# Attention output by token: four heads in every step, or sixteen heads once a sequence

## The chip, the cores and the metric

The kernel runs on one core of one Trainium2 chip. The metric is the device time in microseconds of one execution; the time of a kernel is the median of several runs. All numbers in the profile are of one further, profiled execution.

## What is computed

One decoder layer for 16 sequences of 256 tokens with 256 channels, in three mixers, each with a layernorm ahead and a residual sum behind it. The change touches the first:

```python
qkv = jnp.einsum('bsd,ndh->bnsh', x, W_qkv)          # 16 heads of 16 channels
q, k, v = jnp.split(qkv, 3, axis=-1)
attn = jnp.einsum('bnqh,bnkh->bnqk', q, k) * scale   # causal mask, softmax over k
out = jnp.einsum('bnqk,bnkh->bnqh', attn, v)
out = out.reshape(B, -1, S)
return jnp.einsum('bds,nhd->bsd', out, W_out)
```

The reshape reads the heads' outputs in another order than the sums that follow, so W_out enters as one factor per row of the reshaped tensor, and the output has to be re-ordered. The second mixer is a gated linear attention over a context (scores times a decay matrix, times values, a norm per head). The third is a mixture of eight experts of which each token takes two.

## The kernel before, in words

Engines: TensorE (PE) multiplies matrices, VectorE (DVE) and ScalarE (ACT) empty PSUM and do the elementwise work, GpSimd (POOL) does selections and indirect DMAs, SyncE (SP) issues most DMAs.

**Order of the work.** First attention alone, then attention with the second mixer of the first eight sequences woven in, then the rest of the second mixer with the experts, then experts only. For the attention and what is woven into it, a list scheduler chooses each engine's order from the program's order and its own estimates of durations; every engine then executes its list in order, and waits at semaphores. From the expert part on, PE, ACT and SP are in the order in which the program is written.

**Attention.** A step k stands for a quad, four of the sixteen heads of one sequence: b, quad = divmod(k, 4). `attend_next(k)` emits: `maxima(k)` (scores ps_s at L370 and L375, and on VectorE twice `less` L384 and `off` L388, then L389, L390 and the transpose L393, whose rows SP copies into the queries); one quarter of the next sequence's preparation (`turn1` with ps_t L191, twice `project` with ps_qk L321, or `project_v` with ps_v L341); `weights(k - 2)` (transposed scores ps_st L411 and L415, exponential on ScalarE L419, causal selection on GpSimd L353); and `values(k - 4)` (ps_av L430 and L435, copied by ScalarE into avt, L439). The steps of a sequence are called first to fourth here: the first has `turn1`, the second and third `project`, the fourth `project_v`.

**by_token.** After the fourth quad's values of a sequence, `by_token(b)` turns all four quads of avt, whose one buffer holds a whole sequence, from channels-by-token to token-by-channel: for each half of 128 tokens four PE transposes into a ps_t tile (ps_o, L448), a reciprocal of the softmax sums (L453, 16 numbers a token), a product with the weights' sums (L454), and a multiplication of 16 x 16 numbers a token into `av` (L455). `av` holds eight sequences and has one buffer.

**reorder.** Behind the eighth sequence, `gather` (L472, L475) and `spread` (L480, L487) transpose av twice and add it to x.

**PSUM.** Pool ps_t has two buffers and serves ps_t, ps_qk, ps_v, ps_av, ps_o and most tiles of the second mixer (its values ps_h among them). Pool ps_p has three buffers of two banks; a step's ps_s takes two, its ps_st two, each taken round in turn.

**The weave.** `for k in range(k0)` runs attention alone. From k0 to `last`, every attend_next(k) is followed by an even share of the steps of gather, spread and the second mixer; they are all given out two steps ahead of `last`.

Of the kernel before, what the change touches and what calls it, by code (L numbers as in the profile page):

```python
# [12 lines left out]
F32 = mybir.dt.float32  # L13
# [3 lines left out]
ALU = mybir.AluOpType  # L17
# [3 lines left out]
P = 128  # L21
B, S, D = 16, 256, 256
NA, HA = 16, 16
NQ = NA // 4
NX, HX = 8, 32
E, FF = 8, 1024
SC = S // P
DC = D // P
FC = FF // P
GB = 8  # L30
UB = 4
TB = 256
HP = 32
# [37 lines left out]
def decoder_layer(  # L71
# [15 lines left out]
    nc = tc.nc  # L87
# [22 lines left out]
    ident = const.tile([P, P], F32, name="ident")  # L110
# [85 lines left out]
    ps_t = ctx.enter_context(tc.tile_pool(name="ps_t", bufs=2, space=PSUM))  # L196
# [25 lines left out]
    att = attention.enter_context(tc.tile_pool(name="att", bufs=2, side="right"))  # L222
# [46 lines left out]
    wq = const.tile([P, SC, NA], F32, name="wq")  # L269
# [22 lines left out]
    seq, quads = {}, {}  # L292
# [3 lines left out]
    def start1(b):  # L296
        mv = lstm.tile([P, SC, 2], F32, tag="mv1", name="mv1")
        rstd = lstm.tile([P, SC], F32, tag="rstd1", name="rstd1")
        statistics(b, mv, rstd)
        xn = lstm.tile([P, SC, D], F32, tag="xn", name="xn", bufs=3)  # L300
        normalized(xn, b, mv, rstd, nc.gpsimd if b else nc.vector)
        seq[b] = {"xn": xn}

    def turn1(b):
        xn = seq[b]["xn"]
        ps = transposed(ps_t, lambda c, dc: xn[:, c, dc * P : (dc + 1) * P])
        xnt = att.tile([P, DC, S], F32, tag="xnt", name="xnt", bufs=1)
        nc.scalar.copy(xnt, ps)  # L308
        seq[b]["xnt"] = xnt

    def project(b, half):


        xnt = seq[b]["xnt"]
        if half == 0:
            seq[b]["qt"] = att.tile([P, NQ, S], F32, tag="qt", name="qt")
        ps = ps_t.tile([P, 2, S], F32, tag="t", name="ps_qk")
        for i in range(2):
            n = (2 * half + i) * 4
            for dc in range(DC):  # L320
                nc.tensor.matmul(  # L321
                    ps[:, i, :],
                    lhsT=wqk_sb[:, dc, n : n + 4].rearrange("p n j h -> p (n j h)"),
                    rhs=xnt[:, dc, :],
                    start=dc == 0,
                    stop=dc == DC - 1,
                )
        part = slice(2 * half, 2 * half + 2)
        nc.scalar.copy(seq[b]["qt"][:, part, :], ps)
        for h in range(4):  # L330
            nc.sync.dma_start(
                out=ks[b % 2][HP * h : HP * h + HA, part, :],
                in_=seq[b]["qt"][HP * h + HA : HP * h + HP, part, :],
            )

    def project_v(b):
        xnt = seq[b]["xnt"]
        ps = ps_t.tile([P, SC, D], F32, tag="t", name="ps_v")
        for c in range(SC):
            for dc in range(DC):  # L340
                nc.tensor.matmul(  # L341
                    ps[:, c, :], lhsT=xnt[:, dc, c * P : (c + 1) * P], rhs=wv_sb[:, dc, :],
                    start=dc == 0, stop=dc == DC - 1,
                )
        nc.scalar.copy(vs[b % 2][:, :, :, :HA], ps.rearrange("p c (n h) -> p c n h", n=NA))

    def rows(h):
        return slice(HP * h, HP * h + HP)
# [53 lines left out]
    def weights(k):  # L402


        b, quad = divmod(k, NQ)
        kt, qt = ks[b % 2], seq[b]["qt"]
        p = att.tile([P, 4, 3 * P], F32, tag="p", name="p", bufs=PB)
        quads[k]["p"] = p
        ps, parts_ = four("ps_st")
        for h in range(4):  # L410
            nc.tensor.matmul(  # L411
                ps[h][:, :S], lhsT=kt[rows(h), quad, :P], rhs=qt[rows(h), quad, :], start=True, stop=True
            )
        for h in range(4):
            nc.tensor.matmul(  # L415
                ps[h][:, S:], lhsT=kt[rows(h), quad, P:], rhs=qt[rows(h), quad, P:], start=True, stop=True
            )
        for part, x_ in parts_:
            nc.scalar.activation(p[:, part, :], x_, AF.Exp, scale=1.0 / math.sqrt(HA))  # L419
        diagonals(p)  # L420

    def values(k):

        b, quad = divmod(k, NQ)
        p, v = quads[k]["p"], vs[b % 2]
        if quad == 0:
            seq[b]["avt"] = att.tile([P, NQ, S], F32, tag="avt", name="avt", bufs=1)
        pa = ps_t.tile([P, S], F32, tag="t", name="ps_av")
        for h in range(4):
            nc.tensor.matmul(  # L430
                pa[rows(h), :], lhsT=v[:, 0, 4 * quad + h, :], rhs=p[:, h, :S], start=True, stop=False,
                tile_position=(0, HP * h), skip_group_check=True,
            )
        for h in range(4):
            nc.tensor.matmul(  # L435
                pa[rows(h), P:], lhsT=v[:, 1, 4 * quad + h, :], rhs=p[:, h, S:], start=False, stop=True,
                tile_position=(0, HP * h), skip_group_check=True,
            )
        nc.scalar.copy(seq[b]["avt"][:, quad, :], pa)  # L439
        del quads[k]  # L440

    def by_token(b):

        avt = seq[b]["avt"]
        for c in range(SC):
            ps = ps_t.tile([P, NA, HP], F32, tag="t", name="ps_o")
            for quad in range(NQ):
                nc.tensor.transpose(  # L448
                    ps[:, 4 * quad : 4 * quad + 4, :].rearrange("p n h -> p (n h)"),
                    avt[:, quad, c * P : (c + 1) * P], ident,  # L450
                )
            rs = att.tile([P, NA], F32, tag="rs", name="rs")
            nc.vector.reciprocal(rs, ps[:, :, HA])  # L453
            nc.vector.tensor_tensor(rs, rs, wq[:, c, :], ALU.mult)  # L454
            nc.vector.tensor_tensor(  # L455
                avs[b // GB][:, c, :, b % GB, :].rearrange("p h n -> p n h"),
                ps[:, :, :HA], rs[:, :, None].to_broadcast([P, NA, HA]), ALU.mult,
            )
        del seq[b]

    def reorder(g):

# [574 lines left out]
    avs = {}  # L1037

    def attend_next(k):


        b, quad = divmod(k, NQ)
        if k < B * NQ:
            maxima(k)
        if b + 1 < B:
            if quad == 0:
                turn1(b + 1)
            elif quad < NQ - 1:
                project(b + 1, quad - 1)
        if 0 <= k - 2 < B * NQ:  # L1050
            weights(k - 2)
        if 0 <= k - 4 < B * NQ:
            done, part = divmod(k - 4, NQ)
            if done % GB == 0 and part == 0:
                avs[done // GB] = big.tile([P, SC, HA, GB, NA], F32, tag="av", name="av")
            values(k - 4)
        if b + 1 < B and quad == NQ - 1:
            project_v(b + 1)
        if 0 <= k - 4 < B * NQ and part == NQ - 1:
            by_token(done)  # L1060
        if quad == NQ - 2 and b + 2 < B:
            start1(b + 2)

# [5 lines left out]
    project_v(0)  # L1069
    output_sums()  # L1070
    nc.vector.tensor_scalar(gain, gain, 1.0, None, ALU.add)
    k0 = GB * NQ + 4
    last = B * NQ + 4

    def take(steps):
        f = steps.pop(0)
# [8 lines left out]
    for k in range(k0):  # L1085
        attend_next(k)
# [18 lines left out]
    for k in range(k0, last):  # L1105
        attend_next(k)
        take_evenly(steps, k + 1 - k0, last - k0 - EARLY)
# [236 lines left out]
```

## Time and profile before

| what | us |
|---|---|
| median of 6 runs (1218.35 to 1230.18) | 1220.68 |
| the profiled execution | 1227.71 |
| its span, first to last instruction | 1225.90 |
| PE busy | 1085.1 (89%) |
| DVE busy | 604.6 (49%) |
| ACT busy | 455.3 (37%) |
| POOL busy | 395.3 (32%) |

| group (L, engine) | count | mean ns |
|---|---|---|
| ps_o L448, PE, 128x128 | 128 | 273 (median) |
| rs L453, DVE, 128x16 | 32 | 257 (median) |
| av L455, DVE, 128x256 | 32 | 599 (median) |
| less L384, DVE, 128x512 | 128 | 678 |
| mxs L389, DVE, 128x1024 to 128x8 | 64 | 1208 |
| avt L439, ACT, 128x256 | 64 | 380 (median) |

A page of the profile gives each engine's busy time, the span in 40 slices, and groups of instructions by line. A timeline lists instructions in order of time; an idle time in brackets says how long the engine waited before one and what ended the wait. Matmuls are pipelined, so the lengths of neighbours overlap, and the starts are what to compare.

### The profile page before, as it was taken

The page shows a single profiled execution, that of the slowest core. Times are in us where ns is not written, and L with a number is a line of the kernel's source. Part 1 is how long each engine was busy: PE and PEld are TensorE (multiplying, and loading weights), DVE is VectorE, ACT ScalarE, POOL GpSimd, SP SyncE. Part 2 cuts the span into 40 slices and gives each one's busy share as a digit, 9 for nine tenths or more (in the row PEclk, how much of TensorE's full clock was granted, in tenths as well). Part 3 has the DMA queues.
Part 4 walks back from the last instruction along what each step waited for, and adds up shares of the span by engine and source line. Part 5 has one row for each costly group of instructions (what it writes and reads, how often), then busy time and mean ns, then how long its engine had stood idle before and what let it go on. Part 6 is the DMA issues. An engine that isn't in the chain of part 4 may idle for free.

```text
span 1225.9 us, 23326 instructions
## 1 busy us (share of the span) xinstructions
PE 1085.1 (89%) x8718; PEld 849.7 (69%) x8718; DVE 604.6 (49%) x1654; ACT 455.3 (37%) x928; POOL 395.3 (32%) x447
## 2 busy tenths in 40 slices
PE   5999999888989898874897859999879999999997
PEld 4677777655656565544675647777758899999996
DVE  4878777666776557525557553573611111111110
ACT  2345444435656552341385423744312111111111
POOL 5233332243534334535131153212542222222222
PEclk9799999978999886868789888999969999999999
DMA  6200000003113100125384455634648887788741
GB/s 189 61 19 13 17 14 17 10 6 109 62 33 126 62 23 27 54 97 217 130 313 149 147 174 182 220 113 138 192 147 298 304 291 248 241 295 258 243 134 22
DMA packets 61233, 165.44 MB, mean 135 GB/s; under 512 B 11584, under 2 KB 42176, under 8 KB 46784
## 3 DMA queue, kind: packets, MB, share of 16 engines
q1 hardware_dynamic: 47328, 144.45, 33.7%
q0 software_dynamic: 13248, 18.69, 7.6%
q8 instruction: 71, 1.16, 0.4%
q10 hardware_dynamic: 544, 0.79, 0.2%
q14 instruction: 42, 0.34, 0.1%
HBM read 136.30 MB, written 23.14 MB: 130 GB/s over the span
## 4 chain that ended last, share of the span: by engine, by line
PE 39%; DMA 13%; issue 10%; DVE 7%; ACT 4%; POOL 4%; another core or an unknown queue 1%; SPq 1%; POOLq 0%; DVEq 0%; ACTq 0%
PE ps_d L1215 11%; DMA out_x<-y,to 10%; PE ps_u L1197 9%; PE ps_h L651 3%; DMA rows<-table 2%; PE ps_t L191 2%; PE ps_sc L628 2%; PE ps_qk L321 2%; PE ps_st L411 2%; PE ps_s L370 1%; PE ps_av L430 1%; POOL out_x L1220 1%; DMA mb<-mm 1%; PE ps_r L1175 1%
## 5 line engine op out<-in xcount | busy, mean ns | idle before, releaser
L1197 PE MATMUL ps_u<-xt,up 128*128 128x128 f32 (+1 forms) x1536 | 258.8, 325 | 11.3 <-issue 9.6
L1215 PE MATMUL ps_d<-down,h 128*128 128x256 f32 x1088 | 254.5, 391 | 0.0
L1197 PEld LDWEIGHTS ps_u<-xt,up 128*128 128x128 f32 x1536 | 228.5, 194 | 36.8 <-issue 17.5
L1220 POOL DMA_INDIRECT out_x<-y,to x68 | 105.3, 1548 | 393.0 <-DVE y L1219 330.1
L1215 PEld LDWEIGHTS ps_d<-down,h 128*128 128x128 f32 x1088 | 210.5, 197 | 30.7 <-issue 2.0
L353 POOL TENSOR_SCALAR_AFFINE_SELECT p<-p 128x512 f32<-128x512 f32 x128 | 78.3, 635 | 200.7 <-ACT p L419 161.9
L419 ACT ACTIVATE p<-ps_st 128x768 f32<-128x768 f32 x128 | 99.1, 810 | 95.2 <-PE ps_st L415 93.9
L1203 ACT ACTIVATE h<-ps_u 128x512 f32<-128x512 f32 x78 | 46.6, 597 | 233.1 <-PE ps_u L1197 199.2
L1219 DVE TENSOR_SCALAR y<-ps_d,wt 128x256 f32<-128x256 f32 x68 | 32.8, 483 | 157.5 <-PE ps_d L1215 136.8
L384 DVE TENSOR_TENSOR less<-mask_a,ps_s 128x512 f32<-128x512 f32 x128 | 86.8, 678 | 42.5 <-PE ps_s L375 40.0
L411 PE MATMUL ps_st<-qt,kt 32*128 32x256 f32 x512 | 81.6, 468 | 24.3 <-DVE off L388 21.9
L370 PE MATMUL ps_s<-kt,qt 16*128 16x256 f32 x512 | 79.9, 440 | 10.8 <-DVE d L637 8.7
L321 PE MATMUL ps_qk<-xnt,wqk_sb 128*128 128x256 f32 x256 | 72.9, 434 | 8.3 <-ACT xnt L308 3.3
L850 POOL DMA_INDIRECT table<-x,place x64 | 63.6, 994 | 47.6 <-DVE place L846 21.6
L389 DVE TENSOR_REDUCE mxs<-less 128x8 f32<-128x1024 f32 x64 | 77.3, 1208 | 0.0
L353 POOL TENSOR_SCALAR_AFFINE_SELECT d<-d 128x512 f32<-128x512 f32 x64 | 39.9, 656 | 114.2 <-ACT d L619 76.8
L637 DVE SCALAR_TENSOR_TENSOR d<-ps_sc,d 128x384 f32<-128x384 f32 (+1 forms) x96 | 60.4, 681 | 23.8 <-PE ps_sc L632 13.8
L411 PEld LDWEIGHTS ps_st<-qt,kt 32*128 32x128 f32 x512 | 36.9, 204 | 50.8 <-issue 37.7
L619 ACT ACTIVATE d<-mb,at 128x256 f32<-128x256 f32 x128 | 63.7, 498 | 15.2 <-DMA mb<-mm 15.1
L182 POOL TENSOR_SCALAR xn<-x,mv,rstd 128x256 f32<-128x256 f32 x46 | 55.7, 1222 | 42.0 <-PE ps_t L191 27.3
L1177 DVE COPY xt<-ps_r 128x256 f32<-128x256 f32 (+1 forms) x48 | 25.6, 532 | 87.9 <-PE ps_r L1175 85.8
L321 PEld LDWEIGHTS ps_qk<-xnt,wqk_sb 128*128 128x128 f32 x256 | 52.2, 214 | 20.6 <-issue 3.8
(236 smaller groups left out, 1610.9 us busy)
## 6 DMA issues: line engine op xcount, KB each, us to landing
up<-in_wup SPq DMA_DIRECT2D x48, 1024.0 KB
down<-in_wdown SPq DMA_DIRECT2D x48, 1024.0 KB
mb<-mm SPq DMA_DIRECT2D x16, 1024.0 KB
rows<-table SPq DMA_DIRECT2D x20, 265.0 KB
x<-in_x SPq DMA_DIRECT2D x16, 256.0 KB
kt<-qt SPq DMA_DIRECT2D x128, 32.0 KB
qt<-rowed SPq DMA_DIRECT2D x256, 1.0 KB
cin<-in_ctx SPq DMA_DIRECT2D x16, 256.0 KB
```

Source lines behind the costliest of these rows:

```text
L321: nc.tensor.matmul(ps[:, i, :], lhsT=wqk_sb[:, dc, n : n + 4].rearrange("p n j h -> p (n j h)"), rhs=xnt[:, dc, :], start=dc == 0, stop=dc ...
L353: i = nc.gpsimd.affine_select(out=block, in_=block, compare_op=ALU.is_ge, fill=0.0, base=0, pattern=[[0, 4], [1, P]], channel_multiplier=-1,)
L370: nc.tensor.matmul(ps[h // 2][:, h % 2, P : P + S], lhsT=qt[channels(h), quad, P:], rhs=kt[channels(h), quad, :], start=True, stop=True,)
L384: nc.vector.tensor_tensor(less[:, part], mask_a[:, None].to_broadcast([P, 2, SC, P]), p.rearrange("p h (c k) -> p h c k", c=SC)[:, :, :, : ...
L389: nc.vector.tensor_reduce(mx[:, :, :4].rearrange("p c h -> p h c"), less, AX.X, ALU.min)
L411: nc.tensor.matmul(ps[h][:, :S], lhsT=kt[rows(h), quad, :P], rhs=qt[rows(h), quad, :], start=True, stop=True)
L419: nc.scalar.activation(p[:, part, :], x_, AF.Exp, scale=1.0 / math.sqrt(HA))
L619: nc.scalar.activation(d[:, h, :S], mb[:, n, :], AF.Exp, bias=at[:, 0, j, n : n + 1], scale=-1.0)
L850: i = nc.gpsimd.indirect_dma_start(out=table, out_offset=bass.IndirectOffsetOnAxis(ap=place, axis=0), in_=row, in_offset=None, bounds_chec ...
L1197: nc.tensor.matmul(ps[:, j, :], lhsT=m["up"][:, dc, f * P : (f + 1) * P], rhs=m["xt"][:, dc, :t], start=dc == 0, stop=dc == DC - 1,)
L1215: nc.tensor.matmul(ps, lhsT=m["h"][:, f, c * P : (c + 1) * P], rhs=m["down"][:, f, :], start=f == 0, stop=f == FC - 1)
L1220: a = nc.gpsimd.indirect_dma_start(out=acc, out_offset=bass.IndirectOffsetOnAxis(ap=m["to"][:, c : c + 1], axis=0), in_=y, in_offset=None, ...
```

## The change

values(k) writes avt for its own quad alone, into one of two buffers. by_token(k) handles one quad: two transposes, one for each half of the tokens, into one ps_o tile; one reciprocal and one product for both halves (8 numbers a token); and two multiplications of 4 x 16 numbers a token, for each half one. It is emitted in every step, one step behind its values (k - 5), so k0 and `last` grow by one.

```diff
@@ values
-        if quad == 0:
-            seq[b]["avt"] = att.tile([P, NQ, S], F32, tag="avt", name="avt", bufs=1)
+        avt = att.tile([P, S], F32, tag="avt", name="avt", bufs=2)
...
-        nc.scalar.copy(seq[b]["avt"][:, quad, :], pa)
-        del quads[k]
-
-    def by_token(b):
-
-        avt = seq[b]["avt"]
+        nc.scalar.copy(avt, pa)
+        quads[k] = avt
+
+    def by_token(k):
+
+        b, quad = divmod(k, NQ)
+        avt = quads.pop(k)
+        ps = ps_t.tile([P, SC, 4, HP], F32, tag="t", name="ps_o")
         for c in range(SC):
-            ps = ps_t.tile([P, NA, HP], F32, tag="t", name="ps_o")
-            for quad in range(NQ):
-                nc.tensor.transpose(
-                    ps[:, 4 * quad : 4 * quad + 4, :].rearrange("p n h -> p (n h)"),
-                    avt[:, quad, c * P : (c + 1) * P], ident,
-                )
-            rs = att.tile([P, NA], F32, tag="rs", name="rs")
-            nc.vector.reciprocal(rs, ps[:, :, HA])
-            nc.vector.tensor_tensor(rs, rs, wq[:, c, :], ALU.mult)
+            nc.tensor.transpose(ps[:, c].rearrange("p n h -> p (n h)"), avt[:, c * P : (c + 1) * P], ident)
+        part = slice(4 * quad, 4 * quad + 4)
+        rs = att.tile([P, SC, 4], F32, tag="rs", name="rs")
+        nc.vector.reciprocal(rs, ps[:, :, :, HA])
+        nc.vector.tensor_tensor(rs, rs, wq[:, :, part], ALU.mult)
+        for c in range(SC):
             nc.vector.tensor_tensor(
-                avs[b // GB][:, c, :, b % GB, :].rearrange("p h n -> p n h"),
-                ps[:, :, :HA], rs[:, :, None].to_broadcast([P, NA, HA]), ALU.mult,
-            )
-        del seq[b]
+                avs[b // GB][:, c, :, b % GB, part].rearrange("p h n -> p n h"),
+                ps[:, c, :, :HA], rs[:, c, :, None].to_broadcast([P, 4, HA]), ALU.mult,
+            )
+        if quad == NQ - 1:
+            del seq[b]
@@ attend_next
-        if 0 <= k - 4 < B * NQ and part == NQ - 1:
-            by_token(done)
+        if 0 <= k - 5 < B * NQ:
+            by_token(k - 5)
@@ the weave
-    k0 = GB * NQ + 4
-    last = B * NQ + 4
+    k0 = GB * NQ + 5
+    last = B * NQ + 5
```

## The prediction

> **What bounds the kernel now.** I read the page's slices first, then the busy time by stretches, then the instructions of VectorE and of TensorE over one sequence of the early attention, last the waits of the later part.
>
> ```profile
> PE   5999999888989898874897859999879999999997
> DVE  4878777666776557525557553573611111111110
> PEclk9799999978999886868789888999969999999999
> ```
>
> A slice is 30.6 us. Three parts show: up to about 245 us TensorE is at 9 and VectorE at 7 to 8; up to about 545 us no engine is full and the granted clock falls to 6 to 8; after 900 us TensorE alone counts. The stretches put numbers on it (columns: us, then PE, PEld, DVE, ACT, POOL busy with their instruction counts, then the clock, the DMA share, GB/s):
>
> ```profile
> 100.00:150.00 50.00, 48.22 (x560) 35.21 (x558) 38.35 (x88) 24.04 (x44) 17.05 (x24) 1.00 0.08 18
> 300.00:350.00 50.00, 48.48 (x562) 33.26 (x560) 36.00 (x75) 33.37 (x85) 24.14 (x32) 0.92 0.19 63
> 500.00:550.00 50.00, 40.30 (x346) 24.92 (x346) 18.16 (x51) 19.25 (x45) 25.97 (x29) 0.73 0.22 71
> ```
>
> In the attention alone TensorE looks full (48.2 of 50 at clock 1.00), but a busy row hides waits between matmuls, so I took one sequence step by step. VectorE first (start, length, instruction, in brackets the idle time before it):
>
> ```profile
> 118.61 0.69 DVE L384 TENSOR_TENSOR less<-mask_a,ps_s 128x512 f32<-128x512 f32 x1 [0.94 <-PE ps_s L375]
> ...
> 123.22 0.69 DVE L384 TENSOR_TENSOR less<-mask_a,ps_s 128x512 f32<-128x512 f32 x1 [1.04 <-PE ps_s L375]
> ...
> 128.49 0.26 DVE L453 RECIPROCAL rs<-ps_o 128x16 f32<-128x16 f32 x1 [1.71 <-PE ps_o L448]
> 128.79 0.17 DVE L454 TENSOR_TENSOR rs<-rs,wq 128x16 f32<-128x16 f32 x1
> 129.00 0.60 DVE L455 TENSOR_TENSOR av<-ps_o,rs 128x256 f32<-128x256 f32 x1
> ...
> 130.65 0.67 DVE L384 TENSOR_TENSOR less<-mask_a,ps_s 128x512 f32<-128x512 f32 x1
> ```
>
> The last row has no idle time ahead of it: `less` of the next sequence stood behind by_token's six instructions. TensorE in the same stretch:
>
> ```profile
> 123.13 0.70 PE L411 MATMUL ps_st<-qt,kt 32*128 32x256 f32 x4
> 124.39 0.48 PE L411 MATMUL ps_st<-qt,kt 32*128 32x256 f32 x2 [0.56 <-DVE off L388]
> ...
> 127.86 0.60 PE L448 MATMUL ps_o<-ident,avt 128*128 128x128 f32 x4
> 128.39 0.69 PE L370 MATMUL ps_s<-kt,qt 16*128 16x256 f32 x2
> 129.01 0.66 PE L448 MATMUL ps_o<-ident,avt 128*128 128x128 f32 x4
> ...
> 131.04 1.24 PE L411 MATMUL ps_st<-qt,kt 32*128 32x256 f32 x6
> ```
>
> A step without stalls is the second of the sequence, 113.14 to 117.64: ps_s 0.92, ps_qk 1.93, ps_st 0.87, ps_av 0.78. By these lengths the fourth step and the first of the next sequence need 2 x (0.92 + 0.87 + 0.78) + ps_v 1.83 + ps_t 0.58 + ps_o 0.53 and 0.59 = 8.67 us; they take 122.25 to 133.44 = 11.19. The 2.5 us over are 1.24 in the fourth step's ps_st (2.11), 0.56 in ps_s, which the second four transposes cut in two, and 0.74 in the first step's ps_st (1.61). The ps_st waits because its second PSUM tile is the one that `less` and `off` must empty (three tiles for two matmul groups), and `less` is late. A sequence takes 20.30 us (reciprocals at 128.49 and 148.79).
>
> **The change, part by part.** The sum is made against the profiled execution: 1227.71 us, span 1225.90, 1.81 outside it. The median of the six times is 1220.68, 7.03 less; I carry the difference over.
>
> (a) Attention alone, seven periods (reciprocals 67.57 to 210.33). Transposes stay 128, in 64 pairs; I take 0.33 a pair (half of 0.66 for four), 1.32 a sequence for 1.12: +0.2. VectorE does 16 instructions a sequence for 6: four times reciprocal 0.25, multiply 0.17, and two multiplies of 128x64. Those 128x64 are not in the trace with this striding; 0.22 is the row for 128x64 from PSUM (logit<-ps_lt, 218 ns), and a quarter of 0.60 gives 0.15 as the floor. 4 x 0.86 = 3.44 for 2 x 1.03 = 2.06: +1.4 us a sequence. VectorE's idle time there is 0.94 + 1.04 + 1.71 = 3.7, so it still fits. What counts is where it stands. The built order shows reciprocal, multiply, two multiplies directly ahead of every step's `less`, and ps_o at the end of the step or behind the next step's first ps_s matmul. In the first step, by_token's 0.86 then runs beside ps_s's 0.92: `less` can start when ps_s ends. `off` ends 1.0 later (130.65 to 131.65); TensorE has ps_t 0.58 and half of ps_st, 0.4, to do, so some 0.2 of the 1.30 over remain: -1.1. In the second and third steps `less` comes up to 1.1 us late, and ps_qk (1.93) ahead of ps_st covers it with 0.3 to spare. In the fourth the 1.24 stays: its `less` waits for ps_s either way. Net 0.2 - 1.1 = -0.9; seven times, **-6.3**. Ends: -16 if the whole 2.5 went (2.3 x 7), +10 if a narrow multiply cost the 0.60 of the wide one: VectorE's 15.6 busy (38.35 in 50, of 20.3) less 2.1, plus 4 x 1.62, plus its 1.7 of waiting for ps_o is 21.7 us a sequence.
>
> [...] The rows: 128x16 takes 175 ns, 128x256 with the same line's striding 600, so much of a small instruction is fixed. [...] The rows give +22 (1.4 x 16) and, beside them, the idle time that takes it.
>
> (b) Mixing begins one step later (k0 37 for 36), and the attention ends one later: one full step more alone (5.1), one less shared, and the last share of mixing meets a step that has only ps_av and ps_o. A shared step takes 10.9 (four in 290.04 to 333.81), the light ones at the end about 6: 5.1 - 10.9 + 6 = 0.2. Ends: -3, and +5 if mixing's own chain sets the stage's end. I take **+1.5**, for the clock of 0.73 at the end says that chains, not work, set it there.
>
> (c) The one buffer of `av`. by_token of the ninth sequence's first quad now comes ahead of the gathers that read the eighth's: it writes into the buffer they must empty. In the built order its ps_o stands ahead of 30 of the 32 gather transposes, its multiplies behind them all. So one of the two ps_t tiles is held for about a step, and ps_qk, ps_av and the next ps_o take turns in the other, each waiting for ScalarE's copy (0.58, 0.38). Queued behind on VectorE: the next reciprocal, x<-ps_x, `less`. The gathers' 24 transposes took 3.2 us (215.27). **+1.5**, ends 0 and +4.
>
> (d) Shared part, 245 to 545 us. Eight sequences with +1.4 on VectorE are 11 us. The chain of waits gives VectorE 7% of the span, 86 us of 605 busy, one seventh: **+1.5**; ends 0 and +11. ps_t, with two buffers, serves everything here; 16 more tenancies are emptied by VectorE. TensorE waited for `ct`, emptied from the same buffers, 2.4 + 0.6 + 0.2 in seven copies, 0.46 each: at most +7, **+1** taken, since avt is a step old and ACT avt and ACT v (1.1 and 2.0 us of weight-load waits) fall away. The burst ahead of `less` is halved here too: at most 8 x 1.1, **-1.5** taken, for most of these steps wait for other things.
>
> (e) The end: after the last ps_av eight transposes and six VectorE instructions, 541.5 to 543.3, become four and at most eight short ones: **-1**, ends -1.7 and 0. No DMA is added or moved by itself; SP's rows of extras follow `mxs`, which comes up to 1.1 us later in two steps and is used two steps on, and POOL's selections follow ScalarE.
>
> Sum: -6.3 + 1.5 + 1.5 + 1.5 + 1 - 1.5 - 1 = -3.3. Profiled 1224.4, median **1217.4 us**. What follows 545 us waits for the attention's memory and keeps its length: I count the stage's end one for one.
>
> **Rivals.** *Both stages gain* (0.20): if the shared part's waits of ps_st for `off` (15.2 us in 11) go like those of the alone part, -6 more with (b) at 0.2: -10 to -14, 1208.7. For: VectorE idles 20.2 us in seven waits for ps_o there. Against: TensorE is at 48.5 of 50 in 300 to 350 with little to give. *The shared part loses* (0.28): an in-order VectorE reaches a reciprocal before its ps_o is done, twice as often, and the ps_t buffer behind it stops ps_h and ps_qk. Price: 11 + 7 less (a)'s 6.3 and about 3 of overlap, +9: 1229.7. It decides once a shared sequence grows by 0.8 us (6.3 / 8). For: waits of 4.2, 2.7, 2.0 and 7.3 us for ps_o stand in that part now. Against: a step's lag makes ps_o ready early. *It doesn't smooth* (0.10): in the alone part VectorE becomes the loop once a narrow multiply costs 0.4 (15.6 - 2.1 + 4 x 1.22 + 1.7 = 20.1): the period stays 20.3, and (b) to (e) remain: +3, 1223.7. Against: every 128x64 row is under 0.45. My forecast has 0.42, own range 1211 to 1224.
>
> **How the numbers follow.** About 0.5%, 6.1 us, is what a measurement can tell from no change. Faster: the first rival 0.20 and a quarter of the forecast's 0.42, 0.31. Slower: the second rival and a little of the third, 0.30. Between: 0.39. The range reaches from the first rival's far side (1206) over the second's price with two thirds of (b)'s bound, 1232.
>
> **What would show it.** Reciprocal to reciprocal of the same quad in the alone part: 19.4 us for 20.3 (right), 20.3 (third rival). ps_s uncut and ps_st of the first step near 1.1; the fourth step's ps_st still 2.1. 128x64 multiplies near 0.22. First cin transposes within 2 us of now (247.09): (a)'s gain goes into the later begin of (b). Last ps_o at about 539 us for 542.2. I am wrong if a 128x64 multiply costs 0.4 or more, or if the waits for ps_o in the shared part pass 35 us.

## The result and the profile after

The changed kernel takes 1230.67 us against 1222.89 for the kernel before: a ratio of 1.0072, 95% interval 1.0054 to 1.0090. That is slower, by 8 to 9 us (7.8 between the medians, 8.8 by the ratio), where a gain of 3 was forecast. The profiled execution took 1231.74 us, its span is 1230.0 (before: 1227.71 and 1225.9). These two spans lie only 4.1 us apart: the traces show where time moved, and the ratio of the timed executions says how much was lost.

The slices of the page after (30.7 us each):

```profile
PE   5999999998999898976688768999979999999997
DVE  5778888766766756526447553474612111111110
PEclk9799999977988985678799888999969999999999
```

VectorE's digits are nearly those of before. The clock's row has 5, 6, 7 where before has 6, 8, 6, from 460 to 550 us. The busy time by stretches, and then of the whole shared part up to the first of the experts' matmuls (columns: us, then PE, PEld, DVE, ACT, POOL busy with their instruction counts, clock, DMA share, GB/s):

```profile
100.00:150.00 50.00, 47.66 (x568) 33.99 (x566) 41.64 (x115) 24.16 (x44) 17.06 (x24) 1.00 0.08 18
300.00:350.00 50.00, 48.90 (x548) 33.60 (x544) 36.01 (x84) 32.10 (x79) 23.82 (x31) 0.88 0.21 66
500.00:550.00 50.00, 40.28 (x350) 22.61 (x342) 18.98 (x70) 16.30 (x37) 29.93 (x33) 0.67 0.22 76
245.00:560.30 315.30, 278.83 (x2543) 177.38 (x2540) 188.42 (x538) 145.13 (x357) 135.15 (x157) 0.79 0.18 59
```

The same last row of the kernel before, whose shared part ends at 551.9:

```profile
245.00:551.90 306.90, 263.50 (x2568) 175.15 (x2568) 184.41 (x462) 145.40 (x353) 131.22 (x154) 0.82 0.18 60
```

In the first row VectorE has 3.3 us more work in 50, as forecast (1.4 a period of 20.3). By the last row of each kernel the shared part is 8.4 us longer. TensorE's idle time there did not grow, it fell (306.9 - 263.5 = 43.4; 315.3 - 278.8 = 36.5). What grew is its busy time, by 15.3 us, for nearly the same matmuls (2543 records for 2568), and VectorE's by 4.0. The mean granted clock is lower, 0.79 for 0.82. A second execution of the changed kernel, on another chip (after_again below), has the longer part and the busier TensorE too, but not the lower clock:

```profile
245.00:558.80 313.80, 273.87 (x2578) 177.05 (x2577) 192.70 (x551) 146.45 (x359) 135.29 (x157) 0.82 0.18 59
```

**The alone part** gained nothing: 20.39 us a sequence (first matmul of ps_s 149.22 to 169.61) for 20.41 before (148.69 to 169.10). Its steps now take 4.14, 4.44, 5.89 and 5.92; before 5.05, 4.51, 4.66 and 6.19. VectorE over the first step of one sequence:

```profile
149.32 0.21 DVE L450 RECIPROCAL rs<-ps_o 128x8 f32<-128x8 f32 x1 [1.50 <-PE ps_o L447]
149.56 0.17 DVE L451 TENSOR_TENSOR rs<-rs,wq 128x8 f32<-128x8 f32 x1
149.76 0.40 DVE L453 TENSOR_TENSOR av<-ps_o,rs 128x64 f32<-128x64 f32 x2
150.18 0.69 DVE L384 TENSOR_TENSOR less<-mask_a,ps_s 128x512 f32<-128x512 f32 x1
```

The reciprocal starts where the forecast wanted it and `less` 0.86 later: this step gained 0.91. But the gain is not where the forecast had most of it. TensorE in the same step:

```profile
149.22 0.71 PE L370 MATMUL ps_s<-kt,qt 16*128 16x256 f32 x8
...
150.08 0.66 PE L191 MATMUL ps_t<-ident,xn 128*128 128x128 f32 x4
150.67 1.17 PE L411 MATMUL ps_st<-qt,kt 32*128 32x256 f32 x6
...
152.20 0.64 PE L429 MATMUL ps_av<-p,v 128*32 128x256 f32 x8
```

ps_s, no longer cut, and ps_o take 0.86 and 0.37 us for 2.06 together before; ps_st takes 1.53 for 1.62, where the forecast wanted 1.1. The third step lost the gain again. TensorE there, and under it the weight load of the same two transposes:

```profile
157.80 0.69 PE L370 MATMUL ps_s<-kt,qt 16*128 16x256 f32 x2
158.52 0.44 PE L447 MATMUL ps_o<-ident,avt 128*128 128x128 f32 x2
158.88 0.49 PE L370 MATMUL ps_s<-kt,qt 16*128 16x256 f32 x3
...
165.83 0.48 PE L411 MATMUL ps_st<-qt,kt 32*128 32x256 f32 x2 [0.78 <-DVE off L388]
```

```profile
158.51 0.20 PEld L447 LDWEIGHTS ps_o<-ident,avt 128*128 128x128 f32 x2 [0.42 <-ACT qt L329]
```

ps_o needs a ps_t tile that ScalarE's copy `qt` must free (157.88 to 158.46, behind an exponential), and stands in the middle of ps_s: ps_s to ps_qk takes 1.94 us there, for 0.92 uncut and 1.09 in the third step of the kernel before. A second ps_o falls into the same step (163.32 to 163.69). The two, 0.85 and 0.37, are the 1.23 us that this step is longer. The fourth step's ps_st still waits for `off`, as forecast.

**VectorE's waits in the shared part**, from the view of waits, for the changed kernel from 245 to 560 us:

```profile
DVE rs L450 <- PE ps_o L447: 47.5, 19, 6.4
DVE den L674 <- ACT den L673: 11.3, 7, 5.1
DVE r L557 <- ACT r L556: 10.7, 2, 6.4
DVE less L384 <- PE ps_s L375: 10.6, 8, 2.2
```

and for the kernel before, to 552 us:

```profile
DVE rs L453 <- PE ps_o L448: 20.2, 7, 7.3
DVE less L384 <- PE ps_s L375: 14.2, 11, 4.3
```

47.5 us in 19 waits for 20.2 in 7: the prediction's sign of its own failure (35 us) is passed. The last ps_o is at 550.3 us, not 539.

### The profile page after: what moved, and what is told of

The parts are those of the page before. It is cut to its first block, busy times and chain, and to the rows that moved or that the text cites. A ratio compares the mean times of both kernels' runs of the same rounds, so it can differ in the third digit from the quotient of the medians.

```text
span 1230.0 us, 23465 instructions
## 1 busy us (share of the span) xinstructions
PE 1098.3 (89%) x8718; PEld 847.4 (69%) x8718; DVE 619.4 (50%) x1814; ACT 455.6 (37%) x928; POOL 394.9 (32%) x447
## 4 chain that ended last, share of the span: by engine, by line
PE 53%; DMA 16%; issue 10%; DVE 10%; ACT 6%; POOL 3%; another core or an unknown queue 1%; SPq 1%; POOLq 0%; ACTq 0%; DVEq 0%
DMA out_x<-y,to 12%; PE ps_d L1214 9%; PE ps_u L1196 8%; PE ps_qk L321 5%; PE ps_st L411 4%; PE ps_s L370 4%; PE ps_h L650 4%; PE ps_v L341 3%; PE ps_av L429 3%; PE ps_t L191 2%; PE ps_sc L627 2%; PE ps_o L447 2%; DMA rows<-table 2%; PE ps_st L415 1%
## 5 line engine op out<-in xcount | busy, mean ns | idle before, releaser
L1214 PE MATMUL ps_d<-down,h 128*128 128x256 f32 x1088 | 251.7, 388 | 0.0
L384 DVE TENSOR_TENSOR less<-mask_a,ps_s 128x512 f32<-128x512 f32 x128 | 86.9, 679 | 20.2 <-PE ps_s L375 19.7
L370 PE MATMUL ps_s<-kt,qt 16*128 16x256 f32 x512 | 85.5, 464 | 6.5 <-DVE d L636 5.3
```

What stands on the lines that cost most here:

```text
L370: nc.tensor.matmul(ps[h // 2][:, h % 2, P : P + S], lhsT=qt[channels(h), quad, P:], rhs=kt[channels(h), quad, :], start=True, stop=True,)
L384: nc.vector.tensor_tensor(less[:, part], mask_a[:, None].to_broadcast([P, 2, SC, P]), p.rearrange("p h (c k) -> p h c k", c=SC)[:, :, :, : ...
L1214: nc.tensor.matmul(ps, lhsT=m["h"][:, f, c * P : (c + 1) * P], rhs=m["down"][:, f, :], start=f == 0, stop=f == FC - 1)
```

## Experiments

Each is compared with the kernel before on the same chip. They fell on four chips. On two the kernel before takes 1224 to 1227 us, on two 1179 to 1181: the profiled kernels need 630 to 635 us behind the attention on these two, for 670 to 675, whatever the attention did. So ratios are compared, and kernels on one chip above others. `EARLY` (2 in both kernels) is the number of steps ahead of `last` by which the shares are all given out.

### Shift, start and lag, one at a time

**shift_only**: the kernel before, mixing and end one step later.

```diff
-    k0 = GB * NQ + 4
-    last = B * NQ + 4
+    k0 = GB * NQ + 5
+    last = B * NQ + 5
```

> The kernel before, sixteen heads at once, with k0 and last one higher: the weave begins one attention step later and nothing else changes. Theory S (the weave's later begin): the woven mixer's own chain sets the end of the shared part, so a step alone (5.1 us) is added in full: ratio 1.004 to 1.007, first cin transposes 5 us later, periods of the attention alone unchanged at 20.4 us. Theory V (VectorE's ten more short instructions a sequence in the shared part): nothing of them is here, so 0.999 to 1.002. Theory P (twice as many ps_o tiles in the two-buffer pool): 0.999 to 1.002.

Measured 0.9938 [0.9909, 0.9966]: a gain where every theory had none or a loss. The forecast's (b), +1.5, has the wrong sign, and theory S (the later begin itself costs) falls.

**begin36**: the changed kernel with the mixing begun where it was before, in the same 30 shares.

```diff
-    k0 = GB * NQ + 5
+    k0 = GB * NQ + 4
-EARLY = 2
+EARLY = 3
```

> The changed kernel with the weave begun at step 36 again, as before the change, and its shares spread over the same 30 steps; by_token stays by four heads and one step behind. S: the loss goes, ratio 0.997 to 1.002, last ps_o at 541 to 545 us. V and P: the loss stays, 1.005 to 1.009.

Measured 1.0029 [0.9994, 1.0065]: between what S had (up to 1.002) and what V and P had (from 1.005). On this one chip the split is 0.9% behind shift_only; VectorE waits for ps_o 38.7 us in 19.

**split_nolag**: the changed kernel with by_token in its values' own step.

```diff
-        if 0 <= k - 5 < B * NQ:
-            by_token(k - 5)
+        if 0 <= k - 4 < B * NQ:
+            by_token(k - 4)
```

(k0 and `last` as in the kernel before.)

> By four heads, but directly behind the values of the same step; k0 and last as before. S: no shift, 0.998 to 1.003. V and P: all the short instructions and all 64 ps_o tiles are here, 1.005 to 1.009; if only the lag costs, about 1.000. In the attention alone ps_o must wait for ScalarE's avt copy (0.38 us) in each step, unless TensorE has ps_s to do meanwhile.

Measured 1.0339 [1.0287, 1.0391], the alone period 23.2 to 26.7 us, 55.1 us of waits for ps_o in 24. The split without the lag is far worse.

**lag_only**: sixteen heads at once as before, one step later.

```diff
-            seq[b]["avt"] = att.tile([P, NQ, S], F32, tag="avt", name="avt", bufs=1)
+        avt = att.tile([P, S], F32, tag="avt", name="avt", bufs=5)
+        seq[b].setdefault("avt", []).append(avt)
...
-        if 0 <= k - 4 < B * NQ and part == NQ - 1:
-            by_token(done)
+        if 0 <= k - 5 < B * NQ and k % NQ == 0:
+            by_token((k - 5) // NQ)
```

(k0 and `last` one later.)

> Sixteen heads at once as before, but emitted one step later (k0 37, last 69), with five one-quad avt tiles in place of the one of four quads. S: 1.004 to 1.007, as for the weave's later begin alone. V and P: 0.999 to 1.002, for the instructions are those of before.

Measured 0.9891 [0.9852, 0.9930]; no theory had a gain here either. The two parts of the change that are not the split are worth 0.6 to 1.1%, and the split takes more than that.

### Count, time and waits

**after_again**: the changed kernel, beside the next three.

> The changed kernel again, as the reference of the kernels run beside it, for the chip of the first experiments was faster than the first one in the expert part. If the change costs the same there: ratio 1.005 to 1.010 and some 25 us more than the lag alone. Theory S has fallen: the later begin alone gained. Left are V (the short instructions on VectorE), P (an in-order VectorE waits for more ps_o tiles, and ps_t tiles wait for it) and O (the order that the list scheduler arrives at).

Measured 1.0081 [1.0041, 1.0121].

**pairs**: eight heads every second step, with the lag.

```diff
-        ps = ps_t.tile([P, SC, 4, HP], F32, tag="t", name="ps_o")
+        ps = ps_t.tile([P, SC, 8, HP], F32, tag="t", name="ps_o")
...
-        if 0 <= k - 5 < B * NQ:
+        if 0 <= k - 5 < B * NQ and (k - 5) % 2:
```

> Eight heads every second step: half the dose of the change, 8 VectorE instructions a sequence for 6, two ps_o tiles a sequence as before the change, and the lag of one step and k0 37 as changed. V and P: at most a third of the split's cost is left, so near the lag alone, 0.989 to 0.996. O: no order by dose, anywhere from 0.985 to 1.01.

Measured 1.0009 [0.9981, 1.0037], with 18.7 us of waits for ps_o in 7. Half the split lies between the whole and none in time; V and P had 0.989 to 0.996 for it. In waits it is like the kernel before.

**dve_more**: lag_only, with a reciprocal and a multiplication of 8 and 16 columns of avt added in every step; their results are used by nothing.

```diff
+            nc.vector.reciprocal(w, seq[b_]["avt"][q_][:, :8])
+            nc.vector.tensor_tensor(y, seq[b_]["avt"][q_][:, :16], seq[b_]["avt"][q_][:, 64:80], ALU.mult)
```

> The lag alone (sixteen heads), with two short VectorE instructions added in each step that read the avt tile and that nothing uses (8 a sequence, about 1.5 us, as many as the split adds in time). V: the cost of the split comes back without its ps_o tiles: 1.000 to 1.010. P: hardly any, 0.988 to 0.995.

Measured 1.0073 [1.0043, 1.0103], 1.5 to 1.8% above the two measurements of lag_only (on other chips). VectorE in the alone part:

```profile
122.83 0.20 DVE L1063 RECIPROCAL w<-avt 128x8 f32<-128x8 f32 x1 [1.37 <-ACT avt L439]
122.95 0.36 DVE L1064 TENSOR_TENSOR w<-avt 128x16 f32<-128x16 f32 x1
123.23 0.68 DVE L384 TENSOR_TENSOR less<-mask_a,ps_s 128x512 f32<-128x512 f32 x1
```

and its waits from 245 us to the end of the stage:

```profile
DVE w L1063 <- ACT avt L439: 36.3, 19, 6.7
```

No PSUM tile and no matmul was added, so a cost of this size needs no ps_o tile. Instructions whose result nobody reads, and which wait for another engine at the head of VectorE's queue, cost about what the split costs. Not all in the same place: the alone period is 21.35 us here for 20.44 in lag_only, some 6 us in seven sequences, and there the split lost nothing.

**act_evict**: the changed kernel, with ps_o copied to SBUF by ScalarE and VectorE's part one step later.

```diff
+        tok = att.tile([P, SC, 4, HP], F32, tag="tok", name="tok", bufs=2)
+        nc.scalar.copy(tok, ps)
+        quads[k] = tok
+
+    def by_token2(k):
...
+        if 0 <= k - 6 < B * NQ:
+            by_token2(k - 6)
```

(`last` one later, `EARLY` 3.)

> The changed kernel, but ScalarE copies ps_o into SBUF and VectorE's part follows one step later: no VectorE instruction waits for a ps_o tile and none holds one, and all 16 VectorE instructions stay. 64 copies of 0.38 us are added on ScalarE; weave begin at 37 as changed. P: the split's cost goes, 0.985 to 0.998, and the alone period falls under 20 us unless ScalarE's copies come late. V: the cost stays, 1.005 or more.

Measured 1.0186 [1.0149, 1.0223]; the alone period is 24.0 to 24.1 us and VectorE waits 54.0 us in 22 for `tok` in the shared part. The wait was not removed, it changed its name, so this kernel cannot tell P from V.

### The time of the instructions, and the order

**lag_again**: lag_only once more, beside the next three.

> The lag alone (sixteen heads) again, beside the runs below and on their chip: 0.987 to 0.993 if the gain doesn't hang on the chip.

Measured 0.9922 [0.9878, 0.9966].

**dve_own**: lag_only, with two short multiplications in 59 of the steps that read only what VectorE itself wrote; their results are used by nothing.

```diff
+            nc.vector.tensor_tensor(w, mx[:, 0, :8], mx[:, 1, :8], ALU.mult)
+            nc.vector.tensor_tensor(y, mx[:, 0, :16], mx[:, 1, :16], ALU.mult)
```

> The lag alone with two short VectorE multiplications added in each of 59 steps that nothing uses, as before with the ones that read avt, but here they read what VectorE itself has just written in that step (the negated maxima), so they wait for no other engine. V (their time): the 1.8% between the lag alone and the run whose added instructions read avt comes back, 1.003 to 1.010. H (an instruction at the head of VectorE's queue that waits for another engine holds back less, d and all else behind it): at most 0.3% comes back, 0.988 to 0.994.

Measured 0.9982 [0.9944, 1.0020], 12.7 us of waits for ps_o in 5. That is between V (from 1.003) and H (to 0.994). Against lag_again it is 0.6%, some 6 us, with intervals that overlap, for 11.7 us more of VectorE's busy time (612.2 for 600.5); dve_more added 19.8 (621.5 for 601.7 in lag_only). So time alone seems to cost less than waiting, but it isn't shown to cost nothing: at this price the 14.8 us that the split adds to VectorE would be some 8.

**shift2**: the kernel before with k0 and `last` two later.

> The kernel before with the weave begun two steps later (k0 38, last 70). If a later begin helps by itself (less attention beside the mixing), the gain grows or holds, 0.988 to 0.994. O (the order that the list scheduler happens on): 0.985 to 1.01, no trend after 0.994 for one step.

Measured 1.0053 [1.0029, 1.0078]. One step later gains 0.6%, two lose 0.5%.

**early1**: the kernel before with its shares ended one step later.

```diff
-EARLY = 2
+EARLY = 1
```

> The kernel before with the mixing's steps spread over 31 attention steps in place of 30 (EARLY 1), which adds and removes no instruction: it shows how far a mere re-ordering moves the time. O: over 0.5% in either direction. If orders matter little: 0.997 to 1.003.

Measured 0.9854 [0.9808, 0.9899] (0.9911 when measured again, below), with no instruction added or removed. The order in which the scheduler happens to set the same work is worth -1.5 to +0.5%.

### The split in three weaves

All kernels of the split but split_nolag and begin36 begin the mixing one step later than the kernel before (k0 37 for 36). Of those with sixteen heads at once, shift_only and lag_only with all that was made from it do so too; early1 and early3 do not.

**after_early1**: the changed kernel with `EARLY` 1.

> The changed kernel with the mixing spread over 31 steps (EARLY 1), the re-ordering that moved the kernel before to 0.985. If the split costs something of its own beside the luck of the order: 0.990 to 1.000, behind the kernel before in the same weave by 0.5 to 1.5%. If the 0.7% was luck alone: 0.980 to 0.990.

Measured 1.0027 [0.9996, 1.0059], a little above what either theory had.

**after_early3**: the changed kernel with `EARLY` 3.

> The changed kernel with the mixing spread over 29 steps (EARLY 3). A cost of its own: above the kernel before in the same weave (run beside it) by 0.5 to 1.5%. Luck alone: on either side of it.

Measured 1.0056 [1.0031, 1.0081].

**early3**: the kernel before with `EARLY` 3.

> The kernel before with the mixing spread over 29 steps (EARLY 3): a further order of the same instructions. Luck of the order: anywhere from 0.985 to 1.010.

Measured 0.9984 [0.9952, 1.0016], 22.1 us of waits for ps_o in 7, where after_early3 on the same chip has 47.1 in 22.

**before_values**: the changed kernel with by_token emitted ahead of the step's `weights`.

```diff
+        if 0 <= k - 5 < B * NQ:
+            by_token(k - 5)
         if 0 <= k - 2 < B * NQ:
             weights(k - 2)
```

(and not at its old place)

> The changed kernel with by_token(k - 5) emitted ahead of weights(k - 2) in the step, so that ps_o stands between ps_qk (or ps_s) and ps_st and doesn't follow ps_av. If in the attention alone the gain of the first step was lost to ps_o's waits in the second (for the ps_t tile that ScalarE's copy of ps_qk must free) and to the cut ps_s: the period falls from 20.4 to 19.0 to 19.9 us. If VectorE's 16 instructions are the loop there: 20.2 or more. The time as a whole is open to the luck of the order, 0.99 to 1.01.

Measured 1.0301 [1.0244, 1.0358]; the alone period is 21.3 to 22.1 us, where 19.0 to 19.9 was hoped for. TensorE there:

```profile
126.84 0.64 PE L429 MATMUL ps_av<-p,v 128*32 128x256 f32 x8 [1.22 <-DVE av L453]
```

by_token's VectorE part now stands behind the maxima, so it holds a ps_t tile until 126.7, and ps_av waits for it. Its waits of VectorE for ps_o are only 15.3 us in 8, less than before the change: that sum alone does not rank the kernels.

**early1_again** and **lag_early1**: the kernel before, and lag_only, each with `EARLY` 1, on one chip.

> The kernel before with EARLY 1, again: the shares of the second mixer end one step later, so 31 of them for 30, and by_token as before. What is still open is whether its gain (0.9854, on the chip whose expert part is shorter) is a property of the weave or of that chip. Theory O (the order that the scheduler happens on): 0.980 to 0.991 on either chip, stage's end 10 to 20 us ahead of that of the kernel before, waits of VectorE for ps_o in the shared part again 14 to 22 us in 7 or 8. If it was that chip: 0.995 to 1.005. With the changed kernel at 1.0027 in the same weave on the other chip, O with a cost of the split (H, P) has the split at 1.2 to 2.2% here too; if the cost of the split was only luck, the two come within 0.5%.

> Sixteen heads once a sequence as before, one step later, with EARLY 1: the two edits that gained by themselves together (0.9891 and 0.9922; 0.9854). If a gain of each came from its own stall, they add: 0.974 to 0.982. If both are only other orders that the scheduler happens on (O), the sum means nothing: 0.985 to 1.000. H and P expect only that the waits for ps_o stay under 22 us, as in every kernel with sixteen heads at a time, and that it stays ahead of the changed kernel with EARLY 1 (1.0027) by 1% or more.

Measured 0.9911 [0.9881, 0.9940] and 0.9919 [0.9889, 0.9949]. The gains do not add, so they are not two separate stalls removed; orders that happen to suit, or one stall that both edits remove, are left. Both beat both kernels by about 1%, as does lag_only.

### TensorE's clock in all of them

The granted clock is the share of full speed that TensorE was given. Looked at in steps of 1 us, as thirteen of the twenty traces were, it is 1.00 or 0.50, and nothing between but where it changes. The changed kernel, one microsecond a row:

```profile
297.00:298.00 1.00, 0.10 (x2) 0.00 (x0) 0.00 (x0) 1.00 (x5) 0.90 (x2) 1.00 0.01 1
298.00:299.00 1.00, 0.00 (x0) 0.00 (x0) 0.64 (x1) 1.00 (x4) 1.00 (x2) 0.69 0.00 0
299.00:300.00 1.00, 0.54 (x2) 0.53 (x4) 1.00 (x2) 1.00 (x5) 1.00 (x2) 0.50 0.00 0
...
305.00:306.00 1.00, 1.00 (x20) 0.81 (x24) 0.00 (x0) 0.01 (x1) 0.00 (x0) 0.90 0.07 18
```

TensorE stands still for some 2 us, the clock halves within the second one (0.69 is the mean) and comes back 6.8 us later. From 245 us to the end of the shared part, every such stretch in the twenty traces lasts 3.4 us or a multiple (3.4, 6.8, 10.2, 13.6 ...); in the seven others that is read from rows of 5 us. In the changed kernel, from 100 us to 243 us the clock is 1.00 throughout. The longest stretch of the changed kernel:

```profile
466.00:502.00 36.00, 32.38 (x208) 20.19 (x200) 21.66 (x81) 7.07 (x17) 11.34 (x13) 0.50 0.06 20
```

The kernel before has 23.9 us there (from 465), lag_only 20.5.

Not every fall has such a gap ahead of it: at 335.92 the clock fell after 3.4 us (332.50 to 335.92) in which TensorE was busy for 3.31 by its records. That was four 128x128 transposes and, up to the first of ps_av in the last 0.1 us, matmuls of 16 and 32 rows. What makes the clock fall is not shown.

What a microsecond at half clock costs can be estimated from equal programs: over the timed runs of the kernel before on each of the four chips (22 to 29 runs), the span grows by 0.34 to 0.38 us for each us more of it (correlation 0.82 to 0.95). The estimate takes the clock for the cause of this scatter, which no run shows. Time at half clock is here 2 x (1 - mean granted clock) x span. With 0.36 for the price, means over the timed runs, against the kernel before on the same chip:

| kernel | span, us | at half clock, us | x 0.36 | rest |
|---|---|---|---|---|
| after_again | +9.7 | +31 | +11.3 | -1.5 |
| shift_only | -6.9 | -1 | -0.4 | -6.4 |
| lag_only | -13.6 | -11 | -4.0 | -9.6 |
| begin36 | +3.4 | +14 | +5.1 | -1.8 |
| after_early3 | +7.4 | +30 | +10.8 | -3.4 |
| early3 | -2.5 | +18 | +6.6 | -9.1 |
| after_early1 | +3.5 | +31 | +11.1 | -7.6 |
| early1 | -13.3 | -13 | -4.6 | -8.7 |
| early1_again | -11.2 | -15 | -5.4 | -5.8 |
| lag_early1 | -9.0 | +13 | +4.6 | -13.6 |
| pairs | +0.5 | +31 | +11.0 | -10.4 |
| dve_more | +8.7 | +25 | +9.1 | -0.4 |
| dve_own | -2.0 | +2 | +0.6 | -2.6 |
| lag_again | -8.3 | +3 | +1.1 | -9.4 |
| shift2 | +10.1 | +35 | +12.7 | -2.6 |
| act_evict | +21.8 | +19 | +7.0 | +14.8 |
| before_values | +38.5 | +60 | +21.5 | +17.0 |
| split_nolag | +41.0 | +36 | +12.9 | +28.1 |

In each weave the split adds time at half clock: 32 us beside shift_only, 12 beside early3, 43 to 46 beside early1. By the price that is 12, 4 and 16 us, of 17, 10 and 15 to 17 in all. In two other pairs it is less, 15 us for begin36 beside shift_only (one chip) and 18 for after_early1 beside lag_early1 (the same k0 and `EARLY`): by the price 6 of 10 and 7 of 12 us. And the split is not needed for it: shift2, which has sixteen heads at once, adds 35 us; pairs adds 31 and is hardly slower than the kernel before. The last three rows lose by their alone part as well, whose periods grew. This is a reading of runs that were made for other questions: no kernel held the clock fixed, so how much of it is cause, and how much follows from stretches that got longer for another reason, is not separated.

## Why the prediction was wrong

It was of the wrong sign; the second rival, "the shared part loses", with its price of +9, is what came (+0.72% of 1223 is 8.8 us). That its number fits is partly luck: its price counted the gain of 6.3 in the alone part, which did not come. Of its mechanism the first half is in the trace (VectorE waits for ps_o 19 times for 7); the second hardly: in the shared part TensorE and its weight loads waited 9 us for by_token's tile by the profile, ps_h 0.7 of them and ps_qk none.

(a) *Alone, -6.3.* The prices held: a 128x64 multiplication has a median of 262 ns, a pair takes 0.40 from start to end, and the first step gained 0.91 of the 1.1 forecast, though in ps_s and hardly in ps_st. The step that failed is what ps_o costs TensorE, "0.33 a pair". That is the length of two transposes and leaves out the tile and the place: four ps_o tiles a sequence instead of two take turns in a pool of two buffers, and where the scheduler put one between two ps_s matmuls, ps_s took 1.02 more than uncut. The third step's 1.23 ate the first's 0.91. Net 0 for seven sequences, not -6.3. The price for this was in the prediction, in (c), for one sequence only.

(b) *+1.5.* Wrong in sign: shift_only alone gained 0.6%. The kernel before stands in an order that one step of either knob (k0, `EARLY` 1) betters and two steps of k0 make worse (shift2, +0.5%), so the order that the scheduler arrives at outweighs the prices of light and shared steps here. That a clock of 0.73 tells of chains and not of work, for which +1.5 was taken, was the author's estimate and no run shows it: from 466 to 502 us the changed kernel's TensorE is busy 32.4 us of 36 at 0.50.

(c) *+1.5.* Not seen by itself; the first context transposes came at 248.4 for 247.1, within the 2 us forecast.

(d) *Shared part, +1.5 + 1 - 1.5.* The step that failed most. Its three terms priced VectorE's time, the pool and the burst ahead of `less`; together +1. The part from the first context transposes to the experts grew by 7.1 us in the trace (304.8 to 311.9). VectorE's added time there was 4.0 us of busy time; at the price of dve_own that is some 2. "A step's lag makes ps_o ready early" is what was said against the rival: it makes avt ready early, not ps_o, which needs a tile of the pool as well. VectorE stood at the reciprocal in 19 places. One of them, VectorE, then TensorE, then its weight load:

```profile
415.25 0.24 DVE L393 STREAM_TRANSPOSE rowed<-mxs 128x64 f32<-128x64 f32 x1
418.84 0.21 DVE L450 RECIPROCAL rs<-ps_o 128x8 f32<-128x8 f32 x1 [3.35 <-PE ps_o L447]
```

```profile
415.69 1.99 PE L341 MATMUL ps_v<-wv_sb,xnt 128*128 128x256 f32 x8 [0.26 <-ACT avt L438]
417.62 0.70 PE L627 MATMUL ps_sc<-qt,ct 32*128 32x256 f32 x4
418.36 0.44 PE L447 MATMUL ps_o<-ident,avt 128*128 128x128 f32 x2
```

```profile
418.36 0.20 PEld L447 LDWEIGHTS ps_o<-ident,avt 128*128 128x128 f32 x2 [0.45 <-ACT v L345]
```

Its avt was written at 407.21 to 407.59. ps_o stands behind ps_v, which waited for the tile of ps_av, and then waits itself until ScalarE has copied v out of its tile (417.72 to 418.30): 10.8 us after its data it begins, and VectorE has waited 3.35 us. Only some 0.7 of these (0.26 and 0.45) are waits for a tile; for the rest TensorE did other work that its order has ahead of ps_o. So in the whole shared part: ahead of ps_o TensorE and its weight loads waited 11.8 us for ScalarE (3.5 before), VectorE 47.5 for ps_o. And TensorE's clock, which the prediction quoted (0.73 at the end) and took as given, has no term in the sum: in this pair of traces the shared part has 132 us at half clock for 109, by the price above some 8 of its 8.4 us. The second execution, after_again, has 113 and is 6.9 us longer all the same, so the clock is not shown to be the whole of it.

VectorE's busy time in all grew by 14.8 us (604.6 to 619.4), for the 22 worked out from the rows. In the alone part, where 1.3 us a sequence were added, the period did not grow (20.39 for 20.41).

(e) *-1.* The end did not come earlier: the last multiplication of by_token begins at 551.5, for 543.3 before, and the stage ends at 560.3, for 551.9. That a later end of the stage is paid one for one held only roughly: the part behind it kept its length to within 5 us on a chip, and in this pair of traces it was 4.3 us shorter (669.7 for 674.0), so that the spans differ by 4.1 for 8.4.

What is shown: the split costs time in each weave in which it was measured. Its four orders with the lag (the changed kernel, begin36, after_early1, after_early3) measured 1.003 to 1.008, the seven orders with sixteen heads at once and nothing added (the kernel before, shift_only, shift2, early1, early3, lag_only, lag_early1) 0.985 to 1.005, and only shift2 of these is above 1; weave by weave the split costs 0.7 to 1.9%. Shown is also how the alone part lost its gain. What is argued only: why the shared part is longer. VectorE's added time (some 8 us by the price of dve_own, from intervals that overlap), waits at the head of its queue (dve_more is 0.9% above dve_own, on another chip, and mere re-orderings move the kernel by -1.5 to +0.5%), and TensorE's half clock are all left, and no run holds two of them fixed. That the waits are what lowers the clock is not shown: before_values, slowest but one, has 15.3 us of such waits, and pairs has 18.7, as before, with 31 us more at half clock. What stays open besides: what set the clock in each stretch, and differences between chips, which the comparison by ratios may not remove.

## What to carry to other kernels

Cutting a block into four smaller ones, so that each fits a gap, made more places here where VectorE stood and waited (19 waits for 7), and more tenancies of the PSUM pool (four a sequence for two); count these beside the busy time. Before an effect below 1% is believed, move the same instructions by a step or two and see how far the time goes by itself; here that alone (`EARLY` 1, or the lag for sixteen heads) gave 0.985 to 0.992, better than both kernels. Where TensorE's busy time grows for the same matmuls, read its clock microsecond by microsecond ahead of any wait list.

## What the runs showed of the hardware that was not expected

- In these traces the granted clock is 1.00 or 0.50, and in the shared part it stays at half for 3.4 us or a multiple; a digit of 0.7 or 0.8 in a stretch is a share of time, not a speed. Within one program, time at half clock goes with most of the scatter from run to run (correlation 0.82 to 0.95).
- TensorE was near full by its records (32.4 us of 36, from 466 us in the changed kernel) in a stretch of 37.5 us at half clock.
- Chips differ: the same kernel takes 1224 to 1227 us on two and 1179 to 1181 on two others, some 40 of the 45 us behind the attention. Its mean granted clock is 0.916 to 0.917 on the first and 0.931 to 0.932 on the second, 42 us of time at half clock; at the estimated 0.36 that is 15 of the 45 us, and the rest is not explained.
